# Weight loads of GpSimd's DMA queue over 15 instead of 14 DMA engines, in a kernel for all pairs of 32 fields

## The chip, the cores and the metric

The kernel runs on one core of a Trainium2 chip. The metric is the time of one execution in microseconds (us) on the device; lower is better. Each version is executed several times, and the median counts.

## What is computed

There are 1024 samples, each with 32 fields of 128 numbers. For each of the 496 pairs of fields i < j there is a 128x128 weight matrix W[p]. The field i is multiplied by the matrix, and the result element by element by the field j:

```python
v_i = inputs[:, I_IDX, :]                            # (1024, 496, 128)
v_j = inputs[:, J_IDX, :]
transformed = jnp.einsum('bpd,ped->bpe', v_i, W)     # W: (496, 128, 128)
return transformed * v_j                             # float32
```

The output is 496 x 128 x 1024 numbers of four bytes, 260 MB. It leaves the core through the DMA engines, which makes it by far the largest part of what they move.

## The kernel before

**Layout.** The fields stand transposed in HBM, one [128, 1024] block for each field: the 128 numbers lie on partitions, the 1024 samples in a row. The pairs are taken in the order of `_pairs`: i from 30 down to 0, for each i all j above it. Weights come in blocks of eight pairs (`WL = 8`, 62 blocks of 128 partitions x 4 KB = 512 KB); the raw blocks live in a ring of three buffers (`WB = 3`).

**A pair.** Float32 products are made from three products of float32r parts. `split_w` (two pairs at a time) makes the parts of the weights on ScalarE (L141) and GpSimd (L143 to L145), and `split_x` those of a field (L159 to L161, L298). `first` issues two products for each half of 512 samples (L234) and scales what they left in PSUM (L236, ScalarE); `second` adds the third product (L245), and VectorE multiplies by the field j and writes an output tile (L255). The first 15 pairs use plain float32 products (L231).

**Stores.** Four pairs make one output tile of [128, 4, 1024] numbers, 2 MB. ScalarE's queue issues one DMA for it (L282), of 128 rows of 16 KB. `out_tile` (L213) hands out the tile buffers. Three of them (s0, s1, s2) always exist; four more (g0 to g3) are the room of field groups that have not been loaded yet, and drop out one after another as the groups come in, so that the last of the four is gone at about pair 293. VectorE can't write a tile buffer until the store that last used it has landed.

**Loads.** They are issued by a schedule that is written out by hand: one loop over u, half a pair per step (from L264), issues everything. Weight blocks are issued by `load_w`, mostly from the ring at L288 to L295, when a buffer of three has been used up. Blocks with odd numbers and those up to 10 go through SP's hardware queue alone (L125). The 25 even blocks from 12 to 60 (`WAPART`) go through `load_apart`: 112 of the 128 rows (`ROWS = 8 * NE`, `NE = 14`) are issued by GpSimd[...], and the other 16 rows by SP (L108). So that the 112 rows fall on 14 DMA engines with 8 rows each, the source is written as an array whose outermost dimension is 14, and the host has put the rows of these blocks in the order that undoes it.

**The cursor.** [...] `move_on(k)` (L102 to L104) is a tiny transfer, into a tile `mark` that nobody reads[...]:

```python
nc.gpsimd.dma_start(out=mark[: 2 * k], in_=xt[0, : 2 * k, :16].rearrange("(b a) n -> a b n", a=k))
```

It is called once with 5 ahead of the first of the 25 loads (L272), then with `16 - NE`, which is 2, three pairs after each of 24 loads, and with 13 after the last (L277 to L278). [...]

Of the kernel before, what the change touches and what calls it, by code (L numbers as in the profile page):

```python
# [30 lines left out]
XLEAD = 5  # L31

XG = 4
NE = 14
ROWS = 8 * NE
WAPART = tuple(range(12, 62, 2))
BACK = 3
# [13 lines left out]
def kernel(  # L51
# [22 lines left out]
    nc = tc.nc  # L74
# [12 lines left out]
    def load_x(f, pieces=1, eng=None):  # L87
        if f == 0:

            t = rpool.tile([P, WL, P], F32, tag="w", name="x_0").rearrange("p q e -> p (q e)")  # L90
        else:
            t = xpool.tile([P, BT], F32, tag=f"x{f}", name=f"x_{f}")
        s = BT // pieces
        for k in range(pieces):
            (eng or nc.sync).dma_start(out=t[:, k * s : (k + 1) * s], in_=xt[f, :, k * s : (k + 1) * s])
        x_sb[f] = t
# [3 lines left out]
    mark = xpool.tile([32, 16], F32, tag="mark", name="mark")  # L100

    def move_on(k):  # L102

        nc.gpsimd.dma_start(out=mark[: 2 * k], in_=xt[0, : 2 * k, :16].rearrange("(b a) n -> a b n", a=k))  # L104

    def load_apart(dst, src):
        nc.gpsimd.dma_start(out=dst[:ROWS], in_=src[:ROWS].rearrange("(b a) m n -> a b m n", a=NE))
        nc.sync.dma_start(out=dst[ROWS:], in_=src[ROWS:])  # L108
# [3 lines left out]
    def load_group(k, m):  # L112
        if m == XG - 1:
            group[k] = xpool.tile([P, XG, BT], F32, tag=f"g{k}", name=f"x_g{k}")
        f = XG * k + 1 + m
        x_sb[f] = group[k][:, m, :]
        nc.sync.dma_start(out=x_sb[f], in_=xt[f])

    def load_w(c, splits=(0, WL), eng=nc.sync):
        w_raw[c] = rpool.tile([P, WL, P], F32, tag="w", name=f"w_{c}")  # L120
        if c in WAPART:
            load_apart(w_raw[c], wt[c])
            return
        for a, b in zip(splits, splits[1:]):
            eng.dma_start(out=w_raw[c][:, a:b, :], in_=wt[c, :, a:b, :])  # L125
# [97 lines left out]
    def first(u):  # L223
        q, h = divmod(u, 2)
        i, c = pairs[q][0], q // WC
        r = slice(q % WC * P, (q % WC + 1) * P)
        s = slice(h * HB, (h + 1) * HB)
        if h == 0:
            po[q] = ppool.tile([P, BT], F32, tag="po", name=f"po_{q}")
        if q < nq0:  # L230
            nc.tensor.matmul(po[q][:, s], w_raw[q // WL][:, q % WL, :], x_sb[i][:, s], start=True, stop=True)  # L231
        else:
            for t in (0, 1):
                m = nc.tensor.matmul(po[q][:, s], w_s[c][t][:, r], x_s[i][t][:, s], start=t == 0, stop=t == 1)  # L234
                apart(m, scaled.get(u - 1) if h else None)
            scaled[u] = nc.scalar.mul(po[q][:, s], po[q][:, s], 1.0 + EPS)  # L236
            apart(scaled[u], taken.get(q - PB), "TensorE's products, which this waits for, have waited for it")

    def second(u):
        q, h = divmod(u, 2)  # L240
        i, j = pairs[q]
        r = slice(q % WC * P, (q % WC + 1) * P)
        s = slice(h * HB, (h + 1) * HB)
        if q >= nq0:
            m = nc.tensor.matmul(  # L245
                po[q][:, s], w_s[q // WC][2][:, r], x_s[i][2][:, s], start=False, stop=True, skip_group_check=True
            )
            apart(m, scaled[u ^ 1])
        g, k = divmod(q, OG)
        if k == 0 and h == 0:  # L250
            ots[g] = out_tile(g)
        if q >= NQ - 2:
            nc.vector.tensor_tensor(ots[g][:, k, s], po[q][:, s], x_sb[j][:, s], ALU.mult)  # L253
        elif h == 1:
            taken[q] = nc.vector.tensor_tensor(ots[g][:, k, :], po.pop(q), x_sb[j], ALU.mult)  # L255
        if q >= NQ - 2:
            stores.append((u + SLAG, out[g, :, k, s], ots[g][:, k, s]))
        elif g == 0 or q >= NQ - OG:
            if h == 1:
                stores.append((u + SLAG, out[g, :, k], ots[g][:, k]))  # L260
        elif k == OG - 1 and h == 1:
            stores.append((u + SLAG, out[g], ots[g]))

    for u in range(2 * NQ + LAG + SLAG):  # L264
        q = u // 2
        if u < 2 * NQ:
            i, j = pairs[q]
            if u % 2 == 0 and j == i + 1 and XG * ngroup < i - 2 - XLEAD:
                load_x(i - 2 - XLEAD)
            first(u)  # L270
            if u == 2 * nq0:
                move_on(5)  # L272
            if u % 2 == 0 and q in group_at:
                load_group(*group_at[q])
            if u % 2 == 1 and q in w_at:
                load_w(w_at[q])
            if u % 2 == 0 and q in back:  # L277
                move_on(16 - NE if max(w_raw) < WAPART[-1] else 13)  # L278
        if LAG <= u < 2 * NQ + LAG:
            second(u - LAG)  # L280
        while stores and stores[0][0] <= u - LAG:
            nc.scalar.dma_start(*stores.pop(0)[1:])  # L282
        if u % 2 == 1:
            ready = [t for t in todo if t[0] <= q]
            if ready:
                ready[0][2](u)
                todo.remove(ready[0])
        if ring[WB:] and ring[0] in spent:  # L288
            ring.pop(0)
            c = ring[WB - 1]  # L290
            if c == "x":
                load_x(0)
            else:
                load_w(c)
            if c in WAPART:  # L295
                back.append(q + BACK)
        while later and later[0][0] <= u:
            nc.vector.tensor_tensor(*later.pop(0)[1:], ALU.subtract)  # L298
# [31 lines left out]
```

## Time and profile before

| | |
|---|---|
| median of 3 runs | 748.78 us (748.1 to 749.2) |
| the profiled execution's own time | 743.81 us |
| its span, from the first to the last instruction | 742.0 us |
| mean granted TensorE clock | 0.991 |
| moved by the DMA engines | 310.04 MB in 34667 packets, mean 418 GB/s |
| stores of 2 MB: number, median from issue to landing | 122, 13.2 us |
| GpSimd's weight loads of 448 KB: number, median from issue to landing | 25, 11.8 us |
| SP's parts of these blocks, 64 KB: number, median from issue to landing | 25 of 26 such transfers, 6.1 us |
| tiny transfers (`mark`): number, GpSimd's time for one | 26, 637 ns |
| TensorE, VectorE, ScalarE, GpSimd busy | 95%, 86%, 86%, 80% of the span |

The profile is one execution recorded by the hardware. Its page gives the busy time of each engine, the span in 40 slices (of 18.55 us here) with the busy share of the 16 DMA engines in tenths, the DMA queues, and the chain of work that ended last, followed back from the last instruction. The waits say which engine stood still for what, in total, how often and for how long at most. The DMA queues have numbers: q10 is ScalarE's, q1 SP's and q0 GpSimd's[...]. The trace behind the page also has a record of each DMA packet, with queue, start, duration and bytes, but not the DMA engine that moved it.

### The profile page before, as it was taken

The numbers are of one execution on the slowest core, as the hardware profiler recorded it, in microseconds if no ns is written. First come the engines' busy times: TensorE is split into PE (matmuls) and PEld (weight loads), VectorE is DVE, ScalarE is ACT, GpSimd is POOL, SyncE is SP. The second block draws the span as 40 slices with busy tenths as digits, with TensorE's granted clock in tenths as the row PEclk, the third lists the DMA queues.
The fourth block names the chain that finished last, engine by engine and source line by source line (L and its number), as shares of the span: only waits on it lengthen the run. The fifth ranks groups of instructions, "written<-read, shape, count | busy, mean of one in ns | idle before, by whom it ended". The sixth has DMA issues, their size and how long they took to land.

```text
span 742.0 us, 10650 instructions
## 1 busy us (share of the span) xinstructions
PE 703.8 (95%) x2946; PEld 549.4 (74%) x2946; DVE 636.8 (86%) x550; ACT 634.9 (86%) x1256; POOL 594.8 (80%) x882
## 2 busy tenths in 40 slices
PE   7999999999999999999899979999999999999994
PEld 3577777777878887776687758867878778777783
DVE  4888999999999998987798868977999899888885
ACT  1298999999999999898899968988989999998893
POOL 1789999999999999887778866977797878797660
PEclk9999999999999999999999999999999999999998
DMA  9999999999999999999999998999999999999998
GB/s 347 427 424 428 427 427 425 430 423 426 427 419 426 423 424 425 425 423 422 425 428 422 428 423 334 420 423 423 423 425 422 426 423 415 430 421 422 424 408 351
DMA packets 34667, 310.04 MB, mean 418 GB/s; under 512 B 5296, under 2 KB 5424, under 8 KB 18992
## 3 DMA queue, kind: packets, MB, share of 16 engines
q10 hardware_dynamic: 19584, 261.10, 83.4%
q1 hardware_dynamic: 10592, 36.77, 12.3%
q0 software_dynamic: 4432, 11.48, 3.9%
q8 instruction: 24, 0.39, 0.2%
q14 instruction: 35, 0.29, 0.1%
HBM read 49.29 MB, written 260.05 MB: 417 GB/s over the span
## 4 chain that ended last, share of the span: by engine, by line
PE 61%; DMA 23%; DVE 8%; POOL 3%; issue 2%; ACT 1%; DVEq 0%; ACTq 0%; POOLq 0%
PE po L234 38%; DMA out_dram<-ot 23%; PE po L245 19%; DVE ot L255 6%; PE po L231 4%; DVE xd L298 2%; POOL wd L145 1%; POOL wl L143 1%; POOL xl L160 1%; ACT po L236 0%; DMA x<-in_xt_dram 0%; POOL xl L161 0%; POOL wd L144 0%; DVE ot L253 0%; ACT wh L141 0%
## 5 line engine op out<-in xcount | busy, mean ns | idle before, releaser
L236 ACT ACTIVATE po<-po 128x512 f32<-128x512 f32 x962 | 553.4, 584 | 76.3 <-PE po L234 60.3
L255 DVE TENSOR_TENSOR ot<-po,x 128x1024 f32<-128x1024 f32 x358 | 429.8, 1220 | 70.9 <-DMA out_dram<-ot 23.8
L234 PE MATMUL po<-xh,wh 128*128 128x512 f32 x962 | 382.4, 398 | 20.1 <-DVE ot L255 19.1
L245 PE MATMUL po<-xd,wd 128*128 128x512 f32 x962 | 376.3, 391 | 4.8 <-DVE ot L253 2.4
L234 PE MATMUL po<-xl,wl 128*128 128x512 f32 x962 | 377.1, 392 | 1.4 <-POOL wl L143 1.0
L234 PEld LDWEIGHTS po<-xh,wh 128*128 128x128 f32 x962 | 181.2, 188 | 78.3 <-DVE ot L255 41.7
L143 POOL TENSOR_TENSOR wl<-w,wh 128x256 fp32r<-128x256 f32 x241 | 185.2, 768 | 66.1 <-ACT wh L141 60.0
L245 PEld LDWEIGHTS po<-xd,wd 128*128 128x128 f32 x962 | 181.1, 188 | 45.2 <-DVE ot L253 3.2
L234 PEld LDWEIGHTS po<-xl,wl 128*128 128x128 f32 x962 | 181.3, 188 | 41.0 <-POOL wl L143 4.0
L145 POOL TENSOR_TENSOR wd<-wl,wd 128x256 fp32r<-128x256 f32 x241 | 181.4, 753 | 20.1
L255 DVE TENSOR_TENSOR ot<-po,x_g 128x1024 f32<-128x1024 f32 x136 | 164.0, 1222 | 25.9 <-DMA out_dram<-ot 9.7
L144 POOL TENSOR_SCALAR wd<-wh 128x256 fp32r<-128x256 f32 x241 | 101.9, 423 | 20.5
L141 ACT ACTIVATE wh<-w 128x256 fp32r<-128x256 f32 x241 | 98.7, 410 | 5.7 <-DVE ot L255 3.6
L298 DVE TENSOR_TENSOR xd<-xh,xl 128x512 fp32r<-128x512 f32 x52 | 48.5, 934 | 0.0
L160 POOL TENSOR_TENSOR xl<-x_g,xh 128x512 fp32r<-128x512 f32 x32 | 41.5, 1297 | 3.2 <-ACT xh L159 2.9
L160 POOL TENSOR_TENSOR xl<-x,xh 128x512 fp32r<-128x512 f32 x20 | 25.8, 1290 | 15.7 <-ACT xh L159 15.4
L161 POOL TENSOR_SCALAR xl<-xl 128x512 fp32r<-128x512 f32 x52 | 34.4, 662 | 4.6
L231 PE MATMUL po<-x,w 128*128 128x512 f32 x60 | 28.4, 630 | 3.9 <-DMA x<-in_xt_dram 3.9
L231 PEld LDWEIGHTS po<-x,w 128*128 128x128 f32 x60 | 11.6, 199 | 19.9 <-issue 13.7
L159 ACT ACTIVATE xh<-x 128x512 fp32r<-128x512 f32 x20 | 12.3, 624 | 11.4 <-DMA x<-in_xt_dram 11.3
L159 ACT ACTIVATE xh<-x_g 128x512 fp32r<-128x512 f32 x32 | 20.0, 624 | 0.0
L104 POOL DMA_DIRECT2D mark<-in_xt_dram x26 | 16.6, 637 | 0.0
(7 smaller groups left out, 19.9 us busy)
## 6 DMA issues: line engine op xcount, KB each, us to landing
out_dram<-ot ACTq DMA_DIRECT2D x122, 2048.0 KB, 13.2
w<-in_wt_dram SPq DMA_DIRECT2D x36, 512.0 KB, 11.1
w<-in_wt_dram POOLq DMA_DIRECT2D x25, 448.0 KB, 11.8
x_g<-in_xt_dram SPq DMA_DIRECT2D x16, 512.0 KB, 17.0
x<-in_xt_dram SPq DMA_DIRECT2D x14, 512.0 KB, 9.5
out_dram<-ot ACTq DMA_DIRECT2D x6, 512.0 KB, 8.3
w<-in_wt_dram SPq DMA_DIRECT2D x26, 64.0 KB, 6.1
x<-in_xt_dram ACTq DMA_DIRECT2D x4, 256.0 KB, 5.7
```

Source lines behind the costliest of these rows:

```text
L141: halved[c] = nc.scalar.mul(h, raw, 1.0 - 2.0**-13)
L143: nc.gpsimd.tensor_tensor(l, raw, h.bitcast(F32), ALU.subtract)
L144: nc.gpsimd.tensor_scalar(d, h.bitcast(F32), EPS, 1.0, ALU.mult, ALU.mult)
L145: nc.gpsimd.tensor_tensor(d, l.bitcast(F32), d.bitcast(F32), ALU.subtract)
L160: nc.gpsimd.tensor_tensor(l, x_sb[f][:, s], h.bitcast(F32), ALU.subtract)
L161: nc.gpsimd.tensor_scalar(l, l.bitcast(F32), 1.0 / EPS, 1.0, ALU.mult, ALU.mult)
L231: nc.tensor.matmul(po[q][:, s], w_raw[q // WL][:, q % WL, :], x_sb[i][:, s], start=True, stop=True)
L234: m = nc.tensor.matmul(po[q][:, s], w_s[c][t][:, r], x_s[i][t][:, s], start=t == 0, stop=t == 1)
L236: scaled[u] = nc.scalar.mul(po[q][:, s], po[q][:, s], 1.0 + EPS)
L245: m = nc.tensor.matmul(po[q][:, s], w_s[q // WC][2][:, r], x_s[i][2][:, s], start=False, stop=True, skip_group_check=True)
L255: taken[q] = nc.vector.tensor_tensor(ots[g][:, k, :], po.pop(q), x_sb[j], ALU.mult)
L298: nc.vector.tensor_tensor(*later.pop(0)[1:], ALU.subtract)
```

## The change

The rows of the 25 weight blocks that GpSimd issues become 120 of 128, over 15 DMA engines with 8 rows each; SP's part shrinks from 16 rows (64 KB) to 8 (32 KB). The first move of the cursor is by 4 instead of 5, and the one after each load by 1 instead of 2. For k = 1 the tiny transfer takes another form: one element of four bytes. [...] The last move stays at 13[...]. The host's reordering follows `NE` and `ROWS`. Nothing else differs.

```diff
-NE = 14
+NE = 15
 ROWS = 8 * NE
...
     def move_on(k):
 
-        nc.gpsimd.dma_start(out=mark[: 2 * k], in_=xt[0, : 2 * k, :16].rearrange("(b a) n -> a b n", a=k))
+        if k == 1:
+            nc.gpsimd.dma_start(out=mark[:1, :1], in_=xt[0, :1, :1])
+        else:
+            nc.gpsimd.dma_start(out=mark[: 2 * k], in_=xt[0, : 2 * k, :16].rearrange("(b a) n -> a b n", a=k))
...
             if u == 2 * nq0:
-                move_on(5)
+                move_on(4)
```

## The prediction, made before the changed kernel was run

> **What bounds the kernel now.** First I read the 40 slices of the page and its DMA queues.
>
> ```profile
> PE   7999999999999999999899979999999999999994
> ...
> DMA  9999999999999999999999998999999999999998
> ...
> q10 hardware_dynamic: 19584, 261.10, 83.4%
> q1 hardware_dynamic: 10592, 36.77, 12.3%
> q0 software_dynamic: 4432, 11.48, 3.9%
> ```
>
> The DMA engines are full from end to end: the three queues alone take 99.6% of 16 engines' time, 83.4 of them for the stores. TensorE is nearly as full (95%). Next come the waits, and pieces of the chain around 350 and 670 us (start, length, what):
>
> ```profile
> PEld po L234 <- DVE ot L255: 41.7, 58, 5.8
> DVE ot L255 <- DMA out_dram<-ot: 33.5, 32, 6.3
> PE po L234 <- DVE ot L255: 19.1, 24, 5.4
> ```
>
> ```profile
> 347.37 21.18 DMA out_dram<-ot
> ...
> 677.58 12.33 DMA out_dram<-ot
> ```
>
> VectorE waits 33.5 us for stores to land, and TensorE for VectorE. A store waits up to 21 us in the first part, where more than three tile buffers exist, and about 12 later. [...] By stages (us, busy time of each engine, granted clock, DMA share, GB/s):
>
> ```profile
> 124.00:290.00 166.00, 164.58 (x712) 132.07 (x711) 154.00 (x134) 155.26 (x311) 152.99 (x226) 1.00 1.01 425
> 290.00:440.00 150.00, 141.15 (x601) 110.76 (x599) 123.07 (x108) 132.66 (x262) 123.90 (x187) 1.00 1.01 424
> 452.00:690.00 238.00, 231.80 (x1001) 185.99 (x1000) 208.10 (x178) 216.71 (x430) 194.76 (x295) 1.00 1.01 420
> ```
>
> TensorE has 1% to spare in the first, 6% in the second, 3% in the third; DMA has none in any.
>
> **Which engine is the slowest.** The trace's packet records don't name the DMA engine. But on one engine a packet begins 3 to 4 ns before the last one's recorded end, so I linked them into 16 rows, for the stretches (trace's clock, 10.4 us ahead of the span's) 38 to 215, 246 to 330, 520 to 570 and 645 to 690 us. Two rows get no weight rows of q0: the spared engines.
> - On 14 rows and on one spared one, a store's 16 KB packet takes 611 ns (median), a 4 KB packet 159.
> - On the other spared one, call it A, it takes 635 and about 165: 4% slower, from the start, before any load of q0. Against the pack A falls from even to 3 us behind by 125 us.
> - The ordinary spared one, B, becomes slower (mean up to 650) in bursts once it leads; I take that as no loss of its own.
>
> [...] If right, the change spares B and loads A, the slow one.
>
> [...]
>
> **The change part by part.**
> - *Eight rows more on the fifth engine, 25 times.* 25 x 8 = 200 packets x (165 - 3.5) ns = 32.3 us if it is A, 31.1 if ordinary. Eight 4-byte packets per load that a spared engine runs now (9 ns each) go: -1.1 us.
> - *SP's part: 8 rows instead of 16.* [...]
> - *Cursor.* As many moves as before, on GpSimd 637 ns each and 622 for a load. Lower bound: nothing changes. Upper: 120/112 of a load's issue, 45 ns x 25 = 1.1 us. I take 0.5: GpSimd is 80% busy and on the chain for about 3% of it, so its work hides under TensorE; uncovered it would be those 1.1 us. [...] SP's issue is 0.33 us as before, on a queue that mostly waits. No wait is added.
>
> How much of A's 31 us counts? A's own work in the first part (124 to 440 us): 57 stores x 8 x 0.6315 = 288 us, 190 load packets x 0.1615 = 31, other 2: 321 us in 316, and indeed its lag grows from 14 to 18 us after issue. No slack: 14 loads x 1.29 = 18 us more. Its backlog is at the buffers' limit (17 to 21 us), so VectorE waits that much longer. After the 8 us gap at 440 us, where three buffers are left and A catches up: 50 stores x 5.05 = 253, 139 packets = 22, small stores, semaphores and fetches 7: 282 us in 291. There are 9 us of slack (A leads there), and 11 loads x 1.29 = 14, so 5 us more. Sum +23 us. From below: none of the bursts and the stall remain, 16 of the 619 us from 122 us of the span to the end aren't A's own work, so 32 - 16 = +16, and with milder bursts on a loaded engine some us less: +14. From above, nothing hides: +31. On the profiled execution: 743.8 + 23 = 767. The median of the runs is 5.0 us above that execution (748.78), so I add 23 to it: 772 us, 3.1% slower; range of this case 763 to 780.
>
> **The rivals.**
> 1. *A loaded, but less of it counts* (chance 0.12): A's 4% is partly the profiled execution's own, or TensorE's limit covers more. Then +3 to +14, say 757. For: TensorE is at 99% in one stage. Against: 4% appears in every stretch.
> 2. *The spared one is A* (0.13): if the order of the two is the other way round. The newly loaded B then carries what the 14 ordinary engines carry; 743.8 + 0 and 748.8. For: the order is inferred only. [...]
> 3. *Faster* (0.05): [...]: 745. [...]
> 4. *The four bytes don't move the cursor* (inside the main case, 0.05): [...]; A is loaded 23 or 24 times of 25: +21.5, 770, not told apart by the time.
> 5. *Worse than 783* (0.02)[...].
>
> **How the numbers follow.** The main case with rival 4 has 0.68, which gives 772. With rival 1 it comes to 0.80, so the range is 752 to 783, from that rival's lower end to the main case's upper bound (748.8 + 31 + 3 for the spread of runs and a stall). Within 0.2% (about what measurement can tell from no change) is 747.3 to 750.3: most of rival 2, 0.10. Faster: rival 3 and a little of 2, 0.06. Slower: 0.84.
>
> **What would show it.** Right: VectorE's waits for out_dram<-ot rise from 33.5 us to 50 or more, chain pieces after 460 us grow from 12 us, TensorE's share falls, DMA share falls below full on average since 15 engines wait for one; the linked rows show one row without q0 packets, and A with 200 of them and no gaps. Wrong: the row left out is the one with 635 ns (rival 2); a row left out that changes (rival 4); A's packets at 611 ns (rival 1). If the waits stay and the time rises, it is something that I haven't seen.

## The result, and the profile after

The changed kernel takes 758.75 us (median of 4 runs, 758.51 to 759.01), the kernel before 748.44 in the same comparison (744.07 to 749.2): 1.015 times as long, with an interval of 1.0111 to 1.0189, or 10.3 us more by the medians. Ratios, here and below, lie near those of the means (758.75 and 747.54 us here) and leave out runs of over 1.5% above the fastest of their kernel. The forecast was 23 us more. Sign and range held; the size was less than half of it. The two profiled executions are further apart, 743.81 and 758.51 us (spans 742.0 and 756.7): 14.7 us.

The changed kernel's line numbers are 3 higher in the loop (VectorE's L255 is L258, TensorE's L234 is L237). First the slices of its page that answer to those of before, and its DMA queues:

```profile
PE   7999999999999998899899969998999999999994
...
DMA  9999999999999999899999997999999999999997
...
q10 hardware_dynamic: 19584, 261.10, 82.1%
q1 hardware_dynamic: 10192, 35.95, 11.9%
q0 software_dynamic: 4432, 12.30, 4.5%
```

The three queues now fill 98.5% of 16 engines' time where they filled 99.6%. Three slices of the DMA line are below 9 tenths, at 8, 7 and 7, where two were, at 8 each. The packets of q0 are as many as before, 4432, although the loads have 200 packets more; this is taken up below. Next the longest waits:

```profile
DVE ot L258 <- DMA out_dram<-ot: 55.2, 50, 6.6
PEld po L237 <- DVE ot L258: 54.2, 68, 6.1
PE po L237 <- DVE ot L258: 27.8, 37, 5.7
```

VectorE waits for stores 55.2 us instead of 33.5, and TensorE for VectorE 82.0 instead of 60.8 (the two lines added). Of the chain that ended last, 32% is stores instead of 23%. Some pieces of it (start, length, what):

```profile
250.81 23.65 DMA out_dram<-ot
279.49 24.05 DMA out_dram<-ot
...
433.89 17.88 DMA out_dram<-ot
...
702.78 12.47 DMA out_dram<-ot
```

The reader is to see three things: the chain goes through stores from 250 us on (the first piece of over 11 us began at 293 before), the longest of them are 24 us (21 before), and after 460 us they are as long as they were, some 12 us. By stages, with the columns as before:

```profile
124.00:290.00 166.00, 162.58 (x699) 129.53 (x698) 150.99 (x132) 153.06 (x306) 151.58 (x222) 1.00 1.01 423
290.00:440.00 150.00, 139.49 (x587) 110.27 (x586) 121.43 (x107) 128.46 (x254) 117.58 (x177) 0.98 0.99 410
452.00:690.00 238.00, 228.84 (x970) 181.09 (x971) 202.78 (x176) 210.49 (x415) 187.68 (x284) 0.99 0.98 404
```

In the first stage little is lost (423 GB/s against 425). From 290 us on it is 410 against 424 and 404 against 420.

**Which engine is late.** Each store has 16 completions (q10's 2176 four-byte packets are 16 for each of its 136 transfers). Sorted by time they tell whether many of them are late or one. Here are some of the 2 MB stores, the same ones in both kernels (us on the span's clock; "last but one" and "last" are the times from issue to the 15th and the 16th completion):

```
          before                          after
issued   last but one   last      issued   last but one   last     issued later by
176.0       12.7        13.2      176.8       13.8        16.2          0.8
243.6       17.5        17.6      244.4       18.6        24.2          0.8
288.0       18.1        18.4      291.7       15.6        21.8          3.7
312.3       16.2        16.8      322.1        9.2        14.6          9.8
384.5       15.1        17.3      393.3       11.3        18.0          8.8
430.1       14.0        16.4      439.6        9.9        17.0          9.5
530.5       11.6        11.6      540.3       11.6        12.3          9.8
689.1       12.3        12.4      702.8        9.7        12.5         13.7
```

After the change one completion alone is 5 to 7 us behind the other 15 in the rows from 244 to 440 us; before, the last two are at most 2.4 us apart in these rows. And the delay doesn't grow evenly: 0.8 us from the start on, 9 us more between 244 and 312, none in sum from there to 530, then some 4 us, and at the end 14.7.

Which engine is it? I linked the packets into 16 rows, as the prediction had done (a row is an inference from the packets' times). In the kernel before, between 236 and 320 us, 14 rows have 32 weight packets of q0 each, 8 for each of four loads, and two rows have none. One of the two has store packets of 635 ns (median), the other 15 rows have 611. It is called the slow row or the slow engine here. The texts written ahead of the runs call it the fifth engine, and the other row without weight packets the fourth; these are the author's names for two rows, and their places among the engines were not shown. Here is when the slow row was done with a store, and when the last of the other 15 was (us on the span's clock, up to the last packet):

```
                 slow row   last of the other 15   last of the 16
before, 114.1      127.7           125.8           the slow one
before, 254.5      272.3           272.7           another
before, 341.3      359.5           362.0           another
before, 423.8      438.0           441.1           another
after,  244.4      268.1           262.6           the slow one
after,  297.1      318.0           310.4           the slow one
```

After the change the slow row ends the stores. Before it, that holds only up to about 200 us. Then it and another take turns, and for all stores issued from 254 to 436 us the last one is an ordinary row, which has 8 packets of every load. The slow row is ahead of it, by 3.1 us at the last store of the table. The stretches that the prediction linked leave out 330 to 520 us, where this lead is largest.

**Which engine each load leaves out.** `move_on` was written to set at which engine the next load begins; the author's word for that place is the cursor. In the linked rows of the changed kernel each load still leaves out one row, but another one each time: of the three loads between 236 and 313 us three rows miss one each (16 weight packets where the other 13 have 24), and the slow row isn't one of them. It is left out once, between 470 and 500 us, where it has no weight packet. So it gets rows of 24 of the 25 loads, and a row left out that changes was the sign that the prediction had named for rival 4. The packets of q0 can be counted without any linking. The kernel before has 66 packets of 128 bytes, as many as the shares into which its 26 tiny transfers are written (5 + 24 x 2 + 13), and 350 of 8 bytes. The changed kernel has 17 of 128 bytes (4 + 13), 15 of 8 bytes, and 1400 of 4 bytes instead of 1216. Without its 24 one-element transfers (the third version below) q0 has 3664 packets, 768 fewer, which is 32 small ones for each. Why the row left out changes along with them, the counts don't show.

### The profile page after: what moved, and what is told of

It is laid out like the page before. It is cut to its first block, busy times and chain, and to the rows that moved or that the text cites. A ratio compares the mean times of both kernels' runs of the same rounds, so it can differ in the third digit from the quotient of the medians.

```text
span 756.7 us, 10650 instructions
## 1 busy us (share of the span) xinstructions
PE 709.3 (94%) x2946; PEld 550.1 (73%) x2946; DVE 633.0 (84%) x550; ACT 636.2 (84%) x1256; POOL 595.0 (79%) x882
## 3 DMA queue, kind: packets, MB, share of 16 engines
q0 software_dynamic: 4432, 12.30, 4.5%
## 4 chain that ended last, share of the span: by engine, by line
PE 51%; DMA 32%; DVE 8%; POOL 4%; issue 2%; ACT 1%; ACTq 0%; DVEq 0%; POOLq 0%
PE po L237 32%; DMA out_dram<-ot 32%; PE po L248 15%; DVE ot L258 6%; PE po L234 4%; DVE xd L301 2%; POOL wd L148 1%; POOL wl L146 1%; POOL xl L163 1%; DMA x<-in_xt_dram 1%; ACT po L239 1%; POOL wd L147 0%; POOL xl L164 0%; DVE ot L256 0%; ACT wh L144 0%
## 5 line engine op out<-in xcount | busy, mean ns | idle before, releaser
L258 DVE TENSOR_TENSOR ot<-po,x 128x1024 f32<-128x1024 f32 x358 | 429.6, 1221 | 85.0 <-DMA out_dram<-ot 35.7
L237 PE MATMUL po<-xh,wh 128*128 128x512 f32 x962 | 384.4, 400 | 28.7 <-DVE ot L258 27.8
L237 PE MATMUL po<-xl,wl 128*128 128x512 f32 x962 | 378.0, 393 | 1.4 <-POOL wl L146 1.0
L237 PEld LDWEIGHTS po<-xh,wh 128*128 128x128 f32 x962 | 181.6, 189 | 91.1 <-DVE ot L258 54.2
L237 PEld LDWEIGHTS po<-xl,wl 128*128 128x128 f32 x962 | 181.7, 189 | 40.3 <-POOL wl L146 4.0
L258 DVE TENSOR_TENSOR ot<-po,x_g 128x1024 f32<-128x1024 f32 x136 | 162.9, 1222 | 29.4 <-DMA out_dram<-ot 19.5
L301 DVE TENSOR_TENSOR xd<-xh,xl 128x512 fp32r<-128x512 f32 x52 | 46.1, 886 | 0.0
L163 POOL TENSOR_TENSOR xl<-x,xh 128x512 fp32r<-128x512 f32 x20 | 25.8, 1291 | 15.6 <-ACT xh L162 15.3
L234 PE MATMUL po<-x,w 128*128 128x512 f32 x60 | 29.2, 644 | 3.9 <-DMA x<-in_xt_dram 3.9
L234 PEld LDWEIGHTS po<-x,w 128*128 128x128 f32 x60 | 11.9, 205 | 20.4 <-issue 14.2
L110 POOL DMA_DIRECT2D w<-in_wt_dram x25 | 16.6, 663 | 0.0
## 6 DMA issues: line engine op xcount, KB each, us to landing
w<-in_wt_dram POOLq DMA_DIRECT2D x25, 480.0 KB, 11.4
```

The source lines that it names most:

```text
L163: nc.gpsimd.tensor_tensor(l, x_sb[f][:, s], h.bitcast(F32), ALU.subtract)
```

## The experiments

All runs were timed in five rounds beside the kernel before, the first four and the last on one chip, the other three on a second one. Theory 1 says that only the slow engine's work counts. Theory 2 is that the number of loaded engines, or the turning of the one left out, costs the time. Theory 3 is that the four-byte transfers cost it, with 32 small packets each.

| version | median, us (lowest to highest) | kernel before beside it | ratio, interval |
|---|---|---|---|
| 15 engines, only the fourth left out | 760.28 (759.92 to 760.5) | 746.84 | 1.0172, 1.0138 to 1.0207 |
| 15 engines, only the fifth left out | 744.69 (742.75 to 749.68) | 746.84 | 0.998, 0.9961 to 1.0 |
| the change without its four-byte transfers | 758.16 (757.71 to 758.28) | 746.84 | 1.0144, 1.0112 to 1.0175 |
| 14 engines, two others left out | 759.79 (759.38 to 760.54) | 746.84 | 1.0168, 1.0136 to 1.02 |
| fifth left out in the first 14 loads, then loaded | 749.68 (748.61 to 750.89) | 747.71 | 1.0025, 1.0013 to 1.0036 |
| fifth loaded in the first 14, then left out | 754.24 (752.39 to 757.65) | 747.71 | 1.0093, 1.0068 to 1.0119 |
| 39 loads, fifth left out | 757.65 (752.68 to 760.66) | 747.71 | 1.0122, 1.0091 to 1.0152 |
| before, with six loads moved forward | 749.53 (744.21 to 759.48) | 747.71 | 1.002, 1.0 to 1.0041 |

### Really sparing only the fourth, and only the fifth

In place of the one element there are two tiny transfers after each load, written as 7 and as 10 shares. The first move is meant to choose the engine that is left out: 4 for the fourth, 5 for the fifth. `mark2` is a second tile that nobody reads.

```diff
-NE = 14
+NE = 15
+    def one_on():
+        move_on(7)
+        move_on(10, mark2)
...
-                move_on(5)
+                move_on(4)
...
-                move_on(16 - NE if max(w_raw) < WAPART[-1] else 13)
+                if max(w_raw) < WAPART[-1]:
+                    one_on()
+                else:
+                    move_on(13)
```

The other version has `move_on(5)` first and `move_on(12)` last.

> Edit: 15 engines as in the change, [...]: two tiny transfers, by 7 and by 10[...], in place of the four bytes, the second into a tile of its own. So each load leaves out the fourth engine, and the fifth, whose packets take 635 ns instead of 611, gets rows of all 25 loads. Theory 1 (the time follows the work of this one slow engine): in the changed kernel it was loaded 24 times of 25, so one load more, +1.3 us: about 760. Theory 2 (what costs is that another engine is left out at each load): 748 to 752. Theory 3 (the four-byte transfers cost the time themselves): 748 to 752 as well.

> Edit: as the kernel with 7 + 10, [...], so that each of the 25 loads leaves out the fifth engine alone and loads the fourth. Theory 1 (only the slow engine's work counts): 744 to 750, as before the change, although 15 engines are used. Theory 2 (15 engines instead of 14, or a fourth engine loaded, cost the time): 757 to 761.

Measured: 760.28 and 744.69 us, 15.6 us apart, with the same number of engines, the same loads and the same instructions (5200 packets of q0 in both). In the linked rows of each trace the same row is left out of every load: in the first it is an ordinary one, and the slow row has 8 packets of each load; in the second it is the slow row, with none. Theory 2 falls. With the slow engine alone left out, 15 engines are no slower than the 14 of before; the upper end of the interval is 1.0, so a gain of some tenths of a per cent is likely but not certain. The chain that ended last in the version with only the fourth left out, and then in the one with only the fifth, by engines:

```profile
PE 59%; DMA 25%; DVE 9%; POOL 2%; issue 2%; ACT 1%; ACTq 0%; DVEq 0%; POOLq 0%
```

```profile
PE 62%; DMA 21%; DVE 9%; POOL 3%; issue 2%; ACT 2%; ACTq 0%; DVEq 0%; POOLq 0%
```

### The change without its four-byte transfers

```diff
-                move_on(16 - NE if max(w_raw) < WAPART[-1] else 13)
+                if max(w_raw) >= WAPART[-1]:
+                    move_on(13)
```

(on the changed kernel, which keeps its first move of 4).

> Edit: the changed kernel without its 24 four-byte transfers. [...] Theory 1: 757.5 to 760, like the changed kernel. Theory 3 (these transfers cost the time, by 16 packets on all engines each): 748 to 752. [...]

Measured: 758.16 us against 758.75 for the change, each beside its own runs of before: 1.0144 and 1.015. So the 24 transfers cost nothing that can be told: GpSimd's time for them, 24 x 0.605 = 14.5 us, is hidden as the prediction had it. Theory 3 falls.

### Fourteen engines, but two others left out

Nothing of the change is made here; only the first and the last move differ from the kernel before. They are meant to leave out two engines other than the fourth and the fifth.

```diff
-                move_on(5)
+                move_on(12)
...
-                move_on(16 - NE if max(w_raw) < WAPART[-1] else 13)
+                move_on(16 - NE if max(w_raw) < WAPART[-1] else 6)
```

> Edit: the kernel before with 14 engines, but the first move by 12 instead of 5 (last 6), [...]. Theory 1: the slow engine gets 200 packets more, as in the changed kernel plus one load: 759 to 763. Theory 2 (14 against 15 engines is what matters): 744 to 750.

Measured: 759.79 us, as with 15 engines. Its longest wait for stores is that of the changed kernel, too:

```profile
DVE ot L255 <- DMA out_dram<-ot: 55.8, 49, 6.6
```

This is the plainest of the runs: two numbers in tiny transfers cost 1.7%, without one packet more (34667 in both). Together with the two versions above, 760.28 and 744.69 us, it says that loading the slow engine decides, and nothing else in the change does.

### The slow engine loaded in one part only

The forecast had split its 23 us into 18 for the 14 loads ahead of the gap at 440 us and 5 for the 11 after it. Here, with `one_on` as above, the engine left out changes after the 14th load. In the first version it is the fifth and then the fourth, in the other one the reverse.

```diff
+    turned = []
...
+                turned.append(q)
+                if len(turned) == len(WAPART):
+                    move_on(13)
+                elif len(turned) == 14:
+                    pass
+                else:
+                    one_on()
```

In the reverse version the first move is 4, the 14th is `move_on(2)`, and the last 12.

> Edit: [...]; the first 14 loads (up to the change from four to three tile buffers at 440 us) leave out the fifth, slow engine, the other 11 the fourth, so the slow one is loaded in the second part alone. In the changed kernel the second part cost 4 us of the 14 to 15 in its profile. Reading of the two traces: 744.7 (fifth left out always) + 4 to 5 = 749. The forecast's split gives 744.7 + 5 = 750, so this run alone doesn't tell them apart. If the slow engine's work counted in full wherever it is put: 11 x 1.29 = 14 more, 759.

> The other way round: the slow engine is loaded in the first 14 loads and left out in the last 11. The forecast's split (no slack in the first part, 18 us) gives 744.7 + 18 = 763. Reading of the two traces (8 us of the first part were slower packets on the engine left out, which go when it is loaded; 9 to 10 us remain): 754 to 756.

Measured: 749.68 and 754.24 us, which is 2.0 and 6.5 us above the runs of before beside them. Against the version with only the fifth left out (2.1 below before) the 11 late loads cost 4.1 us and the 14 early ones 8.7. The 5 us of the forecast for the second part stand; its 18 for the first are twice too many. (The two versions ran on the second chip, and the one with only the fifth left out on the first, so the two costs rest on each version's own runs of before.) The stage 290 to 440 us of the two, in that order, shows where:

```profile
290.00:440.00 150.00, 145.65 (x624) 115.48 (x622) 129.68 (x112) 136.67 (x272) 130.86 (x198) 1.00 1.01 427
```

```profile
290.00:440.00 150.00, 138.50 (x588) 109.85 (x587) 120.77 (x107) 128.32 (x255) 122.60 (x186) 0.98 1.00 413
```

TensorE does 145.65 us of work in 150 where the slow engine has been spared, 138.50 where it has been loaded: 7.2 us of the first part's loss fall into this one stage.

### Sparing the slow engine more often

If each load that goes past the slow engine is worth something, more of them should help. This takes the version with only the fifth left out and makes 39 loads of 25: all blocks from 12 to 39 go through GpSimd.

```diff
-WAPART = tuple(range(12, 62, 2))
+WAPART = (*range(12, 40), *range(40, 62, 2))
```

> A try for a faster kernel: as the one that leaves out the fifth engine alone, with all weight blocks from 12 to 39 over GpSimd's queue instead of every second, then every second to 60 (39 loads instead of 25). It takes 14 x 8 packets, 18 us of work, more off the slow engine in the part where stores land late (17 to 20 us). If the slow engine still sets the waits there: 740 to 743. If ordinary engines or TensorE do by now: 744 to 747, no change. If 14 more software-queue phases slow the others: 748 or more.

Measured: 757.65 us, slower. The waits of this version:

```profile
PEld po L241 <- POOL wl L150: 29.0, 27, 3.2
...
PE po L241 <- POOL wl L150: 17.8, 23, 2.8
...
DVE ot L262 <- DMA out_dram<-ot: 15.2, 18, 2.3
```

Stores are waited for 15.2 us, about half of the least so far (28.3 with only the fifth left out). In their place stand 46.8 us in which TensorE waits for the weight parts that GpSimd makes (under 10 in the versions above). GpSimd issues three DMAs per load, and the tiny ones have become a brake, as two pieces of the chain that ended last show:

```profile
348.92 12.40 DMA mark<-in_xt_dram
361.60 11.27 DMA mark<-in_xt_dram
```

A tiny transfer waits until the earlier one into the same tile has landed, and here that took 11 to 12 us. So in this version the relief of the slow engine ended at GpSimd's time. Whether it would have helped with GpSimd free, no run shows.

### The same 25 loads, at another time

The kernel before again, with six of the 25 loads taken from the second part and given to the stage 290 to 440 us:

```diff
-WAPART = tuple(range(12, 62, 2))
+WAPART = (*range(12, 30, 2), *range(30, 41), 44, 48, 52, 56, 60)
```

> The kernel before with its 25 software-queue loads at other blocks: six of them move from the second part into the stage 290 to 440 us, where GpSimd was busy 124 of 150 us; 14 engines are loaded as before, fourth and fifth left out. If the time is set by the slow fifth engine's backlog of the first part, it is relieved there of 6 x 1.29 = 7.7 us and gets 7.7 us more in the second part, which has some 9 us of room: 741 to 745 us. If ordinary engines or TensorE limit once the slow one is relieved: 745 to 748. If GpSimd's issues or the second part limit: 749 and more.

Measured: 749.53 us, a ratio of 1.002 (1.0 to 1.0041): no gain. In the profile the store issued at 430.1 us in the kernel before comes at 433.3, the one at 460.0 at 462.0, and the first of the series at 36.3 comes at 38.5, as this execution began 2.2 us late. So the first part gained nothing from six loads fewer on the slow engine, and the second part lost 5.8 us (712.0 has become 719.8). The linked packets show why the first part gained nothing: the slow engine isn't the one that ends the stores there. With the store issued at 427.0 us in this run it is done at 436.2, and the last row at 444.3. In the kernel before it is 438.0 and 441.1 for the store issued at 423.8.

The two engines that are left out again and again don't keep all of their relief. In the kernel before, between 236 and 320 us, their store packets take 647 ns (the slow row) and 651 ns (the other) on average, against 611 to 623 on the 14 loaded rows. What makes them slower I can't say. As neither is last from 254 to 436 us, this cost no time there.

## Why the direction was right and the size wrong

**The mechanism.** Right: the slow engine, the fifth, was spared before and is loaded now, and VectorE and then TensorE wait for it (55.2 and 82.0 us). Wrong: that it was already the one waited for in the kernel before (see below). That the change loads this row and spares the other had been inferred only, and the runs bear it out: with the fifth alone left out the time is 744.69 us, with the fourth alone 760.28. Of the signs that the prediction named, the store waits (55.2 us, "50 or more"), the lower TensorE and DMA shares (94% for 95, and 98.5% for 99.6) and a slow row without gaps (none between 240 and 300 us) came. The chain pieces after 460 us did not grow.

**The cursor.** Rival 4's sign is what came, and it had been given 0.05. That a one-element transfer makes the next load leave out the same engine was an assumption that no trace had shown. Measured: another row left out at each of three loads (16 packets against 24) with the one-element copies, the same row at each load with 7 and 10 shares in their place (the slow row has 8 packets of each load in one version and none in the other). For the time it matters little, as said there: 24 of 25 loads reach the slow engine, 1.29 us less than all of them, and the version that loads it every time took 760.28.

**The step that failed: "No slack: 14 loads x 1.29 = 18 us more".** There was slack, of two kinds. First, the sum behind it took 57 stores as the slow engine's own work between 124 and 440 us. The trace has 55 issued there and 54 landed. Second, "its lag grows from 14 to 18 us" was read from each store's last completion, and from 254 us on that is another row's (272.7 against 272.3 us at the first such store, 441.1 against 438.0 at 423.8). The slow engine's own lag is 13.6 us at the store of 114.1 us and 14.2 at the one of 423.8, though it was up to 18 in between.

The same 54 stores, with the forecast's own terms: 54 x 8 x 0.6315 = 272.8, and 31 and 2 more, are 305.8 us of own work. In the kernel before the slow engine took 310.3 us for them (127.7 to 438.0). The other 4.5 us are mostly slower store packets: the mean of these 432 is 648 ns over the 635 of the forecast. And the stretch itself lasted 313.4 us by last completions (128.2 to 441.6), 3.1 more, because another row was last. In the changed kernel the same stretch lasts 323.8 us (128.0 to 451.8), and the slow engine's own work is 305.8 + 18.1 = 323.9. As far as its row can be followed without a doubt, up to 313 us, the mean of its store packets is 635, as their median. So 18.1 us of packets came, 4.5 us of slower packets went, and 3.1 us of lead were used up before anything waited longer:

```
                      own packets   slower packets   ahead of the last   sum    measured
before, 54 stores        305.8           4.5                3.1         313.4     313.4
after, the same 54       323.9           0                  0           323.9     323.8
```

The slower packets are what is left over in the first row; worked out from their mean alone they come to 5.6 us. The forecast had +14 to +16 as its bound from below ("none of the bursts and the stall remain"), and 14.7 between the two profiled executions is inside it. That is in part luck, as the lead over another engine isn't among its terms. The expectation for the run with the slow engine loaded in the first 14 loads hit its 754 to 756 by such luck, too: it put 8 us down to slower packets, which is the sum of the two. What would have corrected the forecast was to count the stores completed and to ask which engine is last.

**"Its backlog is at the buffers' limit (17 to 21 us)".** Wrong as well. In the changed kernel the slow engine's landing rose to 24 us at 244 us with the issue only 0.8 us late. The extra tile buffers took the lag up, and most of it was paid at one place, between 288 and 312 us, where the last of these buffers drops out. The delay rises there from 3.7 to 9.8 us.

**The second part, +5.** Right: from 9.4 us at the store of 460 us to 13.7 at the one of 712, 4.3 us; with the load split in time, 4.1.

**From the execution to the median.** "So I add 23 to it" carried the 5.0 us between the profiled execution and the median over to the changed kernel. It has no such distance: its runs lie within 0.5 us of each other, and its profiled one 0.24 below the median. The runs of the kernel before spread over 743 to 752 us, with one at 756. All versions that load the slow engine in all or nearly all of the loads spread over 0.6 us or less, with another two left out over 1.2; all that spare it in eleven loads or more spread over 2.3 to 9.6, without the two runs at 759 of the last version. No run shows what varies. Of the 13 us by which the forecast was too high, 8.3 come from the size (23 against 14.7) and 4.7 from this step.

**What stays open.** Why engines that are left out of these loads have slower store packets, which was seen in the trace of before (647 and 651 ns) and not switched on and off alone. And whether the kernel before gains if the row that is last in the stage 290 to 440 us is relieved: no version was made for it.

## What to carry to other kernels

Where DMA is full and transfers are spread over all engines, look for the last of the 16 completions of a store: when one alone is late (5 to 7 us here), more work on its engine can cost time (13.4 us against the kernel before beside it, with only the fourth left out), and the same work on another may cost nothing (2.15 us less than before, with only the fifth left out). To cost it, find out first which engine is last, as the slowest need not be (438.0 against 441.1 us here). Then count the work that the engine in question completes between two moments at which it is equally late. Its lead over the last engine is slack, and time that isn't its own work may go when the load comes. And add a cost to the execution that it was worked out from; a median with its own spread is another base.

## What the runs showed of the hardware

- In the packets of the kernel before, linked into 16 rows, one row takes 635 ns for a 16 KB store packet and 164 for a 4 KB packet (medians, 236 to 320 us), and the other 15 take 611 and 159. Leaving it out of 25 loads of 8 packets each was worth 15.6 us of 760 (760.28 and 744.69 us).
- Each 2 MB store has 16 completions. In the kernel before the last was at most 2.4 us behind the last but one in the rows of the table from 244 to 440 us, in the changed kernel 5.4 to 7.1.
- The 24 one-element copies on q0 made 32 small packets each (4432 packets of q0 with them, 3664 without).
- A tiny transfer on q0 needs about as long to land as a whole load (median 9.9 us for the one-element ones, 11.4 for the loads of 480 KB), and the chain of the version with 39 loads has waits of 12.40 and 11.27 us for one.
- The two rows that get no weight packets in the kernel before had slower store packets on average than the 14 that do: 647 and 651 ns against 611 to 623, between 236 and 320 us.
